# A gather-bound relational GNN kernel: paced gathers, other end groups, an earlier start of layer 2, shared node-block transfers

## Chip, cores, metric

The kernel runs on one core of one Trainium2 chip. The metric is the device time of one execution in microseconds; 3947.32 us is the median of ten runs before the change.

## The reference

N = 12500 nodes with C = 128 channels, E = 200000 edges sorted by destination, ten relations. The type of an edge is the argmax of ten of its 42 attributes. Two layers follow, then a residual and a layer norm (no scale or shift):

```python
def _rgcn_layer(x, src, dst, edge_type, w_rel, root, bias):
    N = x.shape[0]
    seg = dst * NUM_REL + edge_type
    xs = x[src]
    sums = jax.ops.segment_sum(xs, seg, num_segments=N * NUM_REL)
    cnt = jax.ops.segment_sum(jnp.ones(seg.shape, x.dtype), seg, num_segments=N * NUM_REL)
    mean = (sums / jnp.maximum(cnt, 1.0)[:, None]).reshape(N, NUM_REL, -1)
    return jnp.einsum('nrd,rdo->no', mean, w_rel) + x @ root + bias
h = jax.nn.relu(_rgcn_layer(x, src, dst, edge_type, w_rel1, root1, b1))
out = _layernorm(x + _rgcn_layer(h, src, dst, edge_type, w_rel2, root2, b2))
```

## The kernel before

The edges are cut into 1563 tiles of 128. A layer goes over them in groups: 95 groups of 16 tiles, then seven end groups of 8, 8, 8, 8, 4, 4 and 3. For each tile GpSimd issues one indirect DMA (L466) that gathers 128 rows of 512 bytes, one for the source of each edge, from x in layer 1 and from the hidden table hD in layer 2. VectorE makes a weighted one-hot matrix `oh` of the tile (L481: relation and place of the destination in a window of 12 nodes, weight one over the count), and TensorE multiplies the two into PSUM (zp, L495). ScalarE copies a group's zp out (zs, L509). For each half of 8 tiles TensorE projects with the ten relation matrices (L521); ScalarE copies (ms, L525 and L527); TensorE places the half's rows into a window of 160 nodes (L537), and VectorE adds that window to `acc`, the transposed node sums, at an offset read from memory (L543). In full groups projection and add run one and two groups behind the gathers; in end groups everything is projected and added at once.

The gathers are queued on GpSimd in tile order. They write a ring of three buffers of 16 tiles (`gpool`). Their completion goes over eight semaphores in turn, so each gather waits for the gather eight places before it, and the first of a group also for TensorE to have finished with its buffer. In full groups the first zp matmul waits for all 16 gathers.

Layer 1 also prepares the edges, in 13 chunks of 128 tiles, as steps between its groups: `sources` (L167) loads and transposes the indices, `types` (L286) loads the attributes in two halves of a chunk of 1.344 MB each (L303, on SyncE's queue, into buffers m0 and m1) and takes the argmax (L279 to L284), writes keys to memory, and `count` (L340) reads them back shifted and counts equal neighbours on VectorE and TensorE (L362 to L366). A half's buffer is loaded again, for the next chunk, once VectorE's L281 has read it.

Nodes are finished in 29 blocks: 23 of 512, then 128s, the last of 84. `done_after` says after which group a block has all its edges. `block_in` (L394) loads x, in layer 2 also hD, through SyncE (`rows_dma`, L392) and transposes it (L407, L409). `block_rows` (L412) adds the bias to the sums (L416), clears `acc` for layer 2 (L418), multiplies with the root matrix (L421) and adds the sums, transposed by a matmul with the identity (L422). `hidden` (L429) applies relu (L435) and stores to hD. `final` (L438) adds the residual x (L447) and normalises (L450 to L457). Layer 2's first gather reads hD, so it waits for the stores of all 29 blocks. In layer 2 a flag is computed (L628 to L640) that sends unusual edge lists to a general path behind the two layers; with these inputs it isn't taken.

Of the kernel before, what the change touches and what calls it, by code (L numbers as in the profile page):

```python
# [20 lines left out]
P = 128  # L21
# [10 lines left out]
RING = 3  # L32
DB = 8
# [10 lines left out]
def rgcn_resnorm_kernel(ctx: ExitStack, tc: tile.TileContext, x, src, dst, attr, w_rel1, root1, b1,  # L44
# [25 lines left out]
    while t < NT:  # L70
        groups.append((t, min(HT if NT - t > 3 * QB else QB, NT - t)))
        t += groups[-1][1]
# [15 lines left out]

    HALF = NT * P - E
    assert C == P and E % GT == 0 and 0 < HALF < P and NT % CT and 1 < groups[-1][1] < groups[-2][1]  # L90
# [27 lines left out]
    wE = keep.tile([P, NCH * CT], F32, name="wE")  # L118

# [46 lines left out]

    def sources(c):  # L167
        p = chunk_rows(c)
        s_i = prep.tile([P, P], I32, name="s_i")
        rows_from(s_i, src, c, 0, P)  # L170
        s_f = prep.tile([P, P], F32, name="s_f")
        early(c, nc.vector.tensor_copy(s_f[:p], s_i[:p]))
        return to_edges(idxE, s_f, c)
# [112 lines left out]
    def types(c):  # L286

        p = chunk_rows(c)
        last = c == NCH - 1
        d_i = prep.tile([P, P + L + 1], I32, name="d_i")  # L290
        if last:
            nc.vector.tensor_copy(d_i[:p, P:], pads[:p])
            q = p - 1
            nc.sync.dma_start(d_i[:q], bass.AP(dst.tensor, dst.offset + c * CE, [[P, q], [1, P + L + 1]]))
            nc.sync.dma_start(d_i[q:p, :P], bass.AP(dst.tensor, dst.offset + E - P, [[P, 1], [1, P]]))
        else:
            rows_from(d_i, dst, c, 0, P + L + 1)
        n = p - 1 if last else p
        ty = prep.tile([P, P], F32, name="ty")
        H = P // 2  # L300
        for o in (0, H):
            m = prep.tile([P, H * D], F32, name=f"m{o // H}")
            d = nc.sync.dma_start(m[:n], bass.AP(attr.tensor, attr.offset + (c * CE + o) * D, [[P * D, n], [1, H * D]]))  # L303
            if last:
                nc.sync.dma_start(m[n:p], bass.AP(attr.tensor, attr.offset + (E - P + o) * D,
                                                  [[P * D, 1], [1, H * D]]))
            if c == 1:
                later(d)
            argmax(c, ty[:p, o:o + H], m[:p].rearrange("p (j d) -> p j d", d=D)[:, :, EMB:EMB + NREL], p, H, prep,
                   riotaP, topP[o // H])  # L310
            yield
        d_f = prep.tile([P, P + L + 1], F32, name="d_f")
        early(c, nc.vector.tensor_copy(d_f[:p], d_i[:p]))
        k = prep.tile([P, P], F32, name="k")
        nc.vector.scalar_tensor_tensor(k[:p], d_f[:p, :P], float(NREL), ty[:p], op0=ALU.mult, op1=ALU.add)
        o = L + c * CE
        nc.sync.dma_start(KD[0, o:o + n * P].rearrange("(p e) -> p e", e=P), k[:n])
        if last:
            nc.sync.dma_start(KD[:, L + E - P + HALF:L + E], k[n:p, HALF:])
        yield  # L320
        key = prep.tile([P, P], F32, name="key")
        nc.vector.tensor_scalar(key[:p], d_f[:p, :P], d_f[:p, 0:1], None, op0=ALU.subtract)
        nc.vector.scalar_tensor_tensor(key[:p], ty[:p], float(WN), key[:p], op0=ALU.mult, op1=ALU.add)
        to_edges(keyE, key, c)
        yield

        bad = prep.tile([P, P], F32, name="bad")
        far = prep.tile([P, P], F32, name="far")
        nc.vector.tensor_tensor(bad[:p], d_f[:p, 1:P + 1], d_f[:p, :P], op=ALU.is_lt)
        nc.vector.tensor_tensor(far[:p], d_f[:p, L + 1:], d_f[:p, :P], op=ALU.is_equal)  # L330
        nc.vector.tensor_tensor(bad[:p], bad[:p], far[:p], op=ALU.max)
        f = prep.tile([P, 2], F32, name="f")
        nc.vector.tensor_reduce(f[:p, 0:1], bad[:p], axis=AX.X, op=ALU.max)
        nc.vector.tensor_tensor(f[:p, 1:2], d_f[:p, P - 1:P], d_f[:p, 0:1], op=ALU.subtract)
        nc.vector.tensor_scalar(f[:p, 1:2], f[:p, 1:2], float(WN) - 0.5, None, op0=ALU.is_gt)
        nc.vector.tensor_reduce(f[:p, 0:1], f[:p], axis=AX.X, op=ALU.max)
        nc.vector.tensor_tensor(fl[:p], fl[:p], f[:p, 0:1], op=ALU.max)
        yield
# [44 lines left out]
    def rows_dma(sb, dr, k, store):  # L383
        n0, n, _ = block(k)
        full = n // P
        pairs = []
        if full:
            pairs.append((sb[:, :full], dr[n0:n0 + full * P, :].rearrange("(t p) c -> p t c", p=P)))
        if n % P:
            pairs.append((sb[:n % P, full], dr[n0 + full * P:n0 + n, :]))  # L390
        for a, b in pairs:
            then("SP", nc.sync.dma_start(b, a) if store else nc.sync.dma_start(a, b))  # L392

    def block_in(k, l):  # L394

        n0, n, subs = block(k)
        last = "e" if k == NBLK - 1 else ""
        b = len(subs) if last else 4
        xb = fin.tile([P, b, C], F32, name="xb" + last)
        rows_dma(xb, x, k, False)  # L400
        fb = xb
        if l:
            fb = fin.tile([P, b, C], F32, name="hb" + last)
            rows_dma(fb, hD, k, False)
        pt = ps_f.tile([P, YB], F32, name="pf")
        for t, h in subs:
            nc.tensor.transpose(pt[:, t * P:t * P + h], fb[:h, t, :], ident[:h, :h])  # L407
        fT = fin.tile([P, b * P], F32, name="fT" + last)
        nc.scalar.activation(fT[:, :n], pt[:, :n], AF.Copy)  # L409
        return xb, fT  # L410

    def block_rows(fT, k, l):  # L412

        n0, n, subs = block(k)
        a = fin.tile([P, YB], F32, name="a")
        nc.vector.tensor_scalar(a[:, :n], acc[:, n0:n0 + n], bsb[l], None, op0=ALU.add)  # L416
        if l == 0:
            nc.vector.memset(acc[:, n0:n0 + n], 0.0)  # L418
        pr = ps_f.tile([P, 4, C], F32, name="pf")
        for t, h in subs:  # L420
            nc.tensor.matmul(pr[:h, t, :], fT[:, t * P:t * P + h], rsb[l], start=True, stop=False)  # L421
            nc.tensor.matmul(pr[:h, t, :], a[:, t * P:t * P + h], ident, start=False, stop=True)  # L422
        return pr
# [5 lines left out]
    def hidden(k, ready):  # L429

        xb, fT = ready
        pr = block_rows(fT, k, 0)
        hb = fin.tile([P, 4, C], F32, name="hb")
        for p, s in spans(k):
            nc.scalar.activation(hb[:p, s], pr[:p, s], AF.Relu)  # L435
        rows_dma(hb, hD, k, True)

    def final(k, ready):  # L438

        xb, fT = ready  # L440
        pr = block_rows(fT, k, 1)
        v = fin.tile([P, 4, C], F32, name="v")
        mv = small.tile([P, 4, 2], F32, name="mv")
        rstd = small.tile([P, 4], F32, name="rstd")
        _, n, subs = block(k)
        for p, s in spans(k):
            nc.vector.tensor_tensor(v[:p, s], pr[:p, s], xb[:p, s], op=ALU.add)  # L447
# [7 lines left out]
        o = fin.tile([P, 4, C], F32, name="o")  # L455
# [3 lines left out]
        rows_dma(o, out, k, True)  # L459
# [3 lines left out]

    def gather(table, t0, n):
        g = gpool.tile([P, G, C], F32, name="g")
        return g, [then("POOL", nc.gpsimd.indirect_dma_start(  # L466
            out=g[:, j, :], out_offset=None, in_=table, in_offset=bass.IndirectOffsetOnAxis(
                ap=idxE[:, t0 + j:t0 + j + 1], axis=0))) for j in range(n)]

    whole = mybir.DependencyInfo(mybir.DependencyClass.Sync, mybir.DependencyReason.DATA)  # L470
# [4 lines left out]
    def ones(k):  # L475

        t0, n = groups[k]
        oh = dpool.tile([P, G, KW], F32, name="oh")
        for j in range(n):
            t = t0 + j  # L480
            then("DVE", nc.vector.tensor_scalar(oh[:, j, :], iotaP[:, :KW], keyE[:, t:t + 1], wE[:, t:t + 1],  # L481
# [4 lines left out]
        return oh, at  # L486

    def sums(table, k, oh, at):
# [4 lines left out]
        zp = ps_z.tile([P, G // QB, YB], F32, name="zp")  # L493
        for j in range(n) if end else reversed(range(n)):
            m = nc.tensor.matmul(zp[:, j // QB, j % QB * KW:(j % QB + 1) * KW], g[:, j, :], oh[:, j, :],  # L495
                                 start=True, stop=True)
# [48 lines left out]
    def layer(table, l, finish, steps, flag_too=False):  # L545
# [8 lines left out]
        def add_oldest():  # L554
# [3 lines left out]
            while done < NBLK and sum(groups[k]) >= done_after(done):  # L558
                finish(done, ready if done == NBLK - 1 else given or block_in(done, l))
# [3 lines left out]
        for k in range(NG):  # L563
            end = k >= NS
            if k and not given and done < NBLK - 1:
                given = block_in(done, l)
            if projected:
                add_oldest()
            if end:
# [4 lines left out]
                if not ready:  # L574
                    ready = block_in(NBLK - 1, l)
# [6 lines left out]
            held.append(sums(table, k, *(made or ones(k))))  # L582
            made = ones(k + 1) if end and k < NG - 1 else None
# [27 lines left out]
    zero = fin.tile([P, YB], F32, name="a")  # L611
    nc.vector.memset(zero, 0.0)
    for a in range(0, NPAD, YB):
        m = min(NPAD - a, YB)
        nc.scalar.activation(acc[:, a:a + m], zero[:, :m], AF.Copy)
# [3 lines left out]
    weights_in()  # L619
    todo = []  # L620
    for c in range(1, NCH):
        s = [as_steps(sources, c + 1)] if c + 1 < NCH else []
        todo.append((c * CT // G - 2, [8 + L // DB + 2], chain(*s, types(c), count(c))))
# [22 lines left out]

    gp = ctx.enter_context(tc.tile_pool(name="gp", bufs=2))
# [120 lines left out]
    with tc.If(flag > 0):  # L768
# [3 lines left out]
        for l, (table, finish) in enumerate(((x, hidden), (hD, final))):  # L772
            nc.vector.memset(acc, 0.0)
# [29 lines left out]
```

## Time and profile before

| | us |
|---|---|
| median of 10 runs (lowest to highest) | 3947.32 (3944.27 to 3949.68) |
| the profiled execution | 3952.98 |
| its span in the profile | 3951.2 |
| first gather of layer 1, last gather of layer 1 | 4.3, 1962.0 |
| first gather of layer 2, last gather of layer 2 | 1973.7, 3928.4 |
| GpSimd busy | 2963.8 (75%) |
| TensorE matmul busy | 2337.4 (59%) |
| VectorE busy | 1512.0 (38%) |
| granted TensorE clock, mean | 0.78 |

How to read it: PE is TensorE, PEld its weight loads, DVE VectorE, ACT ScalarE, POOL GpSimd, SP SyncE; a q behind the name (POOLq, SPq) is that engine's queue of instructions, where DMAs are issued. A group's row gives line, engine and operation, then "output<-inputs", the count, and times; what stands behind "idle" or in brackets is the time in which the engine did nothing before the instruction, and what ended it. "issue" means that the profile shows nothing it waited for. The chain of waits follows the work that ended last backwards, step by step, to what released it. Timeline rows begin with start and duration in us. "DMA to landing" is the time from an issue to the end of its transfer.

### The profile page before, as it was taken

To read this page: it belongs to the slowest core of one execution; us is meant where nothing else is said; L and a number is where in the kernel's file an instruction comes from. 1 tells how busy PE (TensorE), PEld (TensorE's weight loads), DVE (VectorE), ACT (ScalarE), POOL (GpSimd) and SP (SyncE) were. 2 spreads that over 40 slices of the span, in tenths; PEclk is the share of its full clock that TensorE was granted. 3 is DMA by queue.
4 is the path that set the end of the run, shared out by engine and by line. 5 is a ranking of instruction groups with operands and counts; after the bars stand their busy time and mean duration, and the time that the engine had idled before them with its cause. 6 is when DMAs were issued, how large, how long until landed. Compare 5 with 4: busy or idle time off the path is not lost.

```text
span 3951.2 us, 43799 instructions
## 1 busy us (share of the span) xinstructions
PE 2337.4 (59%) x16206; PEld 2245.4 (57%) x16206; DVE 1512.0 (38%) x4660; ACT 528.8 (13%) x1142; POOL 2963.8 (75%) x3142
## 2 busy tenths in 40 slices
PE   4656565565666656656745565555655565556556
PEld 4655555565555555555635565555555555556556
DVE  6444444343444434443323333333333333333333
ACT  2111111111111111111101111111111111111111
POOL 7777777777777777777677777777777777777775
PEclk8777777777777777777877777777777777777778
DMA  5222322222222222221222222222222222222221
GB/s 163 89 73 75 94 59 90 88 65 89 74 74 93 61 89 64 63 62 56 63 58 58 61 69 61 61 61 62 68 61 61 61 69 61 61 61 69 61 59 55
DMA packets 180538, 278.99 MB, mean 71 GB/s; under 512 B 55608, under 2 KB 127175, under 8 KB 177191
## 3 DMA queue, kind: packets, MB, share of 16 engines
q0 software_dynamic: 100032, 205.07, 18.2%
q1 hardware_dynamic: 78577, 71.03, 5.6%
q8 instruction: 132, 2.16, 0.2%
q14 instruction: 89, 0.73, 0.1%
q10 hardware_dynamic: 1708, 0.01, 0.0%
HBM read 262.28 MB, written 13.60 MB: 70 GB/s over the span
## 4 chain that ended last, share of the span: by engine, by line
POOL 66%; issue 24%; DMA 7%; PE 2%; ACT 0%; DVE 0%; POOLq 0%; SPq 0%; ACTq 0%
POOL g L466 66%; DMA g<-in_x_dram,idxE 3%; DMA g<-hD,idxE 3%; PE pp L521 1%; PE zp L495 1%; PE pp L537 0%; ACT zs L509 0%; PE pf L422 0%; PE pf L421 0%; DMA xb<-in_x_dram 0%; POOLq L466 0%; DVE acc L543 0%; DVE a L416 0%; PE pf L407 0%; ACT ms L527 0%
## 5 line engine op out<-in xcount | busy, mean ns | idle before, releaser
L495 PE MATMUL zp<-oh,g 128*128 128x120 f32 x6252 | 1137.8, 358 | 1538.0 <-DMA g<-hD,idxE 789.8
L495 PEld LDWEIGHTS zp<-oh,g 128*128 128x128 f32 x6252 | 1097.3, 271 | 1576.5 <-issue 1474.3
L466 POOL DMA_INDIRECT g<-hD,idxE x1563 | 1478.7, 946 | 487.6 <-issue 470.5
L466 POOL DMA_INDIRECT g<-in_x_dram,idxE x1563 | 1482.4, 948 | 477.2 <-issue 457.7
L481 DVE TENSOR_SCALAR oh<-bank,keyE,wE 128x120 f32<-128x120 f32 x3126 | 1004.0, 400 | 717.4 <-PE zp L495 717.0
L521 PE MATMUL pp<-w,zs 128*96 128x128 f32 x7880 | 898.9, 273 | 17.5 <-ACT zs L509 14.3
L521 PEld LDWEIGHTS pp<-w,zs 128*96 128x96 f32 x7880 | 871.0, 163 | 23.4 <-ACT zs L509 18.5
L509 ACT ACTIVATE zs<-zp 128x480 f32<-128x480 f32 (+1 forms) x782 | 386.0, 575 | 2522.9 <-PE zp L495 2522.6
L543 DVE TENSOR_TENSOR acc<-acc,pp 128x160 f32 x204 | 65.5, 321 | 1390.7 <-PE pp L537 1390.4
L537 PE MATMUL pp<-at,ms 96*128 96x160 f32 (+1 forms) x788 | 210.8, 407 | 6.9 <-ACT ms L527 5.1
L537 PEld LDWEIGHTS pp<-at,ms 96*128 96x128 f32 (+1 forms) x788 | 171.0, 271 | 23.0 <-ACT ms L527 15.9
L527 ACT ACTIVATE ms<-pp 96x256 f32<-96x256 f32 (+1 forms) x198 | 74.5, 376 | 451.0 <-PE pp L521 451.0
L485 DVE TENSOR_SCALAR at<-bank,place 96x160 f32<-96x160 f32 x394 | 133.6, 375 | 0.0
L362 DVE TENSOR_TENSOR eqb<-pf,kh 128x1344 bf16<-128x1344 f32 (+2 forms) x65 | 100.5, 1552 | 75.5 <-PE pf L366 67.9
L422 PE MATMUL pf<-ident,a 128*128 128x128 f32 x392 | 81.4, 291 | 2.1 <-DVE a L416 1.9
L421 PE MATMUL pf<-root,fT 128*128 128x128 f32 x388 | 79.0, 287 | 1.3 <-ACT fT L409 1.3
L422 PEld LDWEIGHTS pf<-ident,a 128*128 128x128 f32 x392 | 64.6, 207 | 3.4 <-DVE a L416 3.1
L421 PEld LDWEIGHTS pf<-root,fT 128*128 128x128 f32 x388 | 62.9, 204 | 2.1 <-ACT fT L409 2.1
L435 ACT ACTIVATE hb<-pf 128x512 f32<-128x512 f32 (+2 forms) x29 | 15.4, 531 | 331.2 <-PE pf L422 329.0
L364 PE MATMUL pf<-eqb,identb 128*128 128x512 bf16 (+2 forms) x130 | 50.5, 389 | 10.6 <-DVE eqb L362 10.6
L366 PE MATMUL pf<-eqb,identb 128*128 128x512 bf16 (+2 forms) x130 | 50.8, 391 | 0.0
L447 DVE TENSOR_TENSOR v<-pf,xb 128x512 f32<-128x512 f32 (+1 forms) x28 | 17.4, 620 | 74.0 <-PE pf L422 73.8
(107 smaller groups left out, 454.7 us busy)
## 6 DMA issues: line engine op xcount, KB each, us to landing
m<-in_edge_attr_dram SPq DMA_DIRECT2D x24, 1344.0 KB
g<-in_x_dram,idxE POOLq DMA_INDIRECT x1563, 2.5
g<-hD,idxE POOLq DMA_INDIRECT x1563, 2.5
xb<-in_x_dram SPq DMA_DIRECT2D x46, 256.0 KB
hD<-hb SPq DMA_DIRECT2D x23, 256.0 KB
hb<-hD SPq DMA_DIRECT2D x23, 256.0 KB
out_dram<-o SPq DMA_DIRECT2D x23, 256.0 KB
w<-in_L_gnn_w_rel_dram SPq DMA_DIRECT2D x2, 640.0 KB
```

What stands on the lines that cost most here:

```text
L362: nc.vector.tensor_tensor(eq[:p], kp[:p, None, :R].to_broadcast([p, DB, R]), fore, op=ALU.is_equal)
L421: nc.tensor.matmul(pr[:h, t, :], fT[:, t * P:t * P + h], rsb[l], start=True, stop=False)
L422: nc.tensor.matmul(pr[:h, t, :], a[:, t * P:t * P + h], ident, start=False, stop=True)
L466: return g, [then("POOL", nc.gpsimd.indirect_dma_start(out=g[:, j, :], out_offset=None, in_=table, in_offset=bass.IndirectOffsetOnAxis(ap= ...
L481: then("DVE", nc.vector.tensor_scalar(oh[:, j, :], iotaP[:, :KW], keyE[:, t:t + 1], wE[:, t:t + 1], op0=ALU.is_equal, op1=ALU.mult))
L485: nc.vector.tensor_scalar(at[:, h, :], iotaP[:HR], place[:, h, k:k + 1], None, op0=ALU.is_equal)
L495: m = nc.tensor.matmul(zp[:, j // QB, j % QB * KW:(j % QB + 1) * KW], g[:, j, :], oh[:, j, :], start=True, stop=True)
L509: then("ACT", nc.scalar.activation(zs[:, :, b * QB:b * QB + m, :], zp[:, b, :m * KW].rearrange("c (j r n) -> c r j n", r=NREL, n=WN), AF.C ...
L521: nc.tensor.matmul(po[:m * WN, h], zs[:, r, h * HT:h * HT + m].rearrange("c j n -> c (j n)"), wsb[l][:, r, :], start=(r == 0), stop=(r == ...
L527: nc.scalar.activation(ms[:, :n // HT], po[:HR, :n // HT], AF.Copy)
L537: nc.tensor.matmul(pa, ms[:m * WN, h], at[:m * WN, h], start=(h == 0), stop=(h == len(parts) - 1))
L543: nc.vector.tensor_tensor(acc[:, s], acc[:, s], pa, op=ALU.add)
```

## The change

1. A gather whose tile number is 6 modulo 8 waits for the landing of the gather three places before it. All gathers are given their order as dependencies without a semaphore.
2. The end groups are 8, 8, 8, 12 and 7 tiles.
3. The first 16 gathers of layer 2 read only the first 12288 rows of hD (`EARLY`, blocks 0 to 26), with indices clamped to them (`idxH`) and weight zero (`wH`) for edges from later rows. What these edges carry is added by eight matmuls (`late_sums`) from the hidden rows of the last two blocks, kept in SBUF (`late_h`), and matrices that `head` prepares at the end of layer 1 (`late_w`).
4. `hidden` also computes layer 2's root product, bias and residual and puts them into `acc`, so layer 2 loads no node blocks and `final` only transposes `acc` and normalises. `acc` starts at b1 in place of zero.
5. Transfers: two blocks of 512 nodes share one load of x, one store to hD and one store of the output (512 KB each); the indices of four chunks share a load; a chunk's attributes come in one load of 2.69 MB in place of two (the first chunk keeps two).

```diff
-        groups.append((t, min(HT if NT - t > 3 * QB else QB, NT - t)))
+        n = NT - t
+        groups.append((t, HT if n > 2 * HT + QB else HT + QB if n > HT + QB else n))
...
+    def of_four(c, a, name, n):
+        if c == 0 or c == NCH - 1:
+            return prep.tile([P, n], I32, name=name)
+        if c % 4 == 1:
+            q = min(4, NCH - 1 - c)
+            four[name] = prep.tile([P, 4, n], I32, name=name + "4")
+            nc.sync.dma_start(four[name][:, :q], bass.AP(a.tensor, a.offset + c * CE, [[P, P], [CE, q], [1, n]]))
+        return four[name][:, (c - 1) % 4]
...
+        m = prep.tile([P, P * D], F32, name="m")
         for o in (0, H):
-            m = prep.tile([P, H * D], F32, name=f"m{o // H}")
-            d = nc.sync.dma_start(m[:n], bass.AP(attr.tensor, attr.offset + (c * CE + o) * D, [[P * D, n], [1, H * D]]))
+            w = H if c == 0 else P
+            if w == H or not o:
+                d = nc.sync.dma_start(m[:n, o * D:(o + w) * D], bass.AP(
+                    attr.tensor, attr.offset + (c * CE + o) * D, [[P * D, n], [1, w * D]]))
...
-    def rows_dma(sb, dr, k, store):
+    def rows_dma(sb, dr, k, store, name=None):
         n0, n, _ = block(k)
+        if k < NPAIR:
+            if k % 2 != store:
+                return
+            n0, n, sb = starts[k - k % 2], 2 * YB, halves_of[name]
...
+    def hidden(k, fT):
+        n0, n, subs = block(k)
+        pr = ps_f.tile([P, 4, C], F32, name="pf")
+        for t, h in subs:
+            nc.tensor.matmul(pr[:h, t, :], fT[:, t * P:t * P + h], rsb[0], start=True, stop=False)
+            nc.tensor.matmul(pr[:h, t, :], acc[:, n0 + t * P:n0 + t * P + h], ident, start=False, stop=True)
+        i = k - (NBLK - 2)
+        hb = late_h[:, i:i + 1] if i >= 0 and not anew else half(k, "hb")
         for p, s in spans(k):
             nc.scalar.activation(hb[:p, s], pr[:p, s], AF.Relu)
+        rows_dma(hb, hD, k, True, "hb")
+        pt = ps_f.tile([P, YB], F32, name="pf")
+        for t, h in subs:
+            nc.tensor.transpose(pt[:, t * P:t * P + h], hb[:h, t, :], ident[:h, :h])
+        hT = fin.tile([P, YB], F32, name="hT")
+        nc.scalar.activation(hT[:, :n], pt[:, :n], AF.Copy)
+        po = ps_f.tile([P, YB], F32, name="pf")
+        nc.tensor.matmul(po[:, :n], rsb[1], hT[:, :n], start=True, stop=True)
+        nc.vector.scalar_tensor_tensor(acc[:, n0:n0 + n], po[:, :n], bsb[1], fT[:, :n], op0=ALU.add, op1=ALU.add)
...
+    def final(k, _):
+        n0, n, subs = block(k)
+        v = ps_f.tile([P, 4, C], F32, name="pf")
...
+        for t, h in subs:
+            nc.tensor.matmul(v[:h, t, :], acc[:, n0 + t * P:n0 + t * P + h], ident, start=True, stop=True)
...
+    def head():
+        nc.vector.tensor_scalar(idxH, idxE[:, :G], EARLY - 1, None, op0=ALU.min)
...
+        for b in range(0, G, QB):
+            pm = [ps_f.tile([P, YB], F32, name="pf") for _ in range(2)]
+            for j in range(QB):
+                t = b + j
+                oh = prep.tile([P, KW], F32, name="ohH")
+                nc.vector.tensor_scalar(oh, iotaP[:, :KW], keyE[:, t:t + 1], wE[:, t:t + 1],
+                                        op0=ALU.is_equal, op1=ALU.mult)
+                for i in range(2):
+                    of = prep.tile([P, P], F32, name=f"of{i}")
+                    nc.vector.tensor_scalar(of, iotaP[:, :P], off[:, i, t:t + 1], None, op0=ALU.is_equal)
+                    nc.tensor.matmul(pm[i][:, j * KW:(j + 1) * KW], of, oh, start=True, stop=True)
...
     def gather(table, t0, n):
         g = gpool.tile([P, G, C], F32, name="g")
+        ix = idxE
+        if is_head(table, t0):
+            table, ix = table[:EARLY, :], idxH
+        for j in range(n):
+            d = then("POOL", nc.gpsimd.indirect_dma_start(
+                out=g[:, j, :], out_offset=None, in_=table, in_offset=bass.IndirectOffsetOnAxis(
+                    ap=ix[:, t0 + j:t0 + j + 1], axis=0)))
+            if (t0 + j) % PACE == PACE - 2 and len(begun) > 2:
+                tc.add_manual_dep(d.ins, begun[-3].ins.name, whole, reason="no more than three under way")
+            if begun:
+                tc.add_manual_dep(d.ins, begun[-1].ins.name, behind, reason="gathers in their order")
+            begun.append(d)
+        return g, begun[-n:]
...
+    def late_sums(table, t0, banks):
+        if is_head(table, t0):
+            for b, z in enumerate(banks):
+                for i in range(2):
+                    n = block(NBLK - 2 + i)[1]
+                    nc.tensor.matmul(z[:, :QB * KW], late_h[:n, i, :], late_w[i][:n, b * QB * KW:(b + 1) * QB * KW],
+                                     start=(i == 0), stop=False)
```

## The prediction

> **What bounds the kernel now.** I read the page's busy shares and its chain of waits first, then the answer for the gather line L466, then the timeline around the turn between the layers, around a load of the edge attributes and at the end. Page, busy shares and chain:
>
> ```profile
> PE 2337.4 (59%) x16206; PEld 2245.4 (57%) x16206; DVE 1512.0 (38%) x4660; ACT 528.8 (13%) x1142; POOL 2963.8 (75%) x3142
> ...
> POOL 66%; issue 24%; DMA 7%; PE 2%; ACT 0%; DVE 0%; POOLq 0%; SPq 0%; ACTq 0%
> ```
>
> POOL and the issue gap before its instructions are 90% of the chain. The gather line says why 75% busy is nevertheless full:
>
> ```profile
> L466 POOL DMA_INDIRECT g<-in_x_dram,idxE x1563: 942/947/1387, 4.3 to 1962.0; - x196
> L466 POOL DMA_INDIRECT g<-hD,idxE x1563: 942/947/1143, 1973.7 to 3928.4; - x196
> ...
>   issue: 928.2, 3010
>   DMA g<-in_x_dram,idxE: 17.4, 57
>   DMA g<-hD,idxE: 16.2, 53
> ...
> DMA to landing us min/median/max: 2.4/2.5/6.8
> ```
>
> A gather takes 0.947 us, and 928.2/3010 = 0.31 us of issue lies before it; so one starts every 1.25 us, 3126 times. The waits on earlier gathers (57 and 53) cost 17.4/57 = 0.31 us each, no more than the ordinary gap: a satisfied wait is free. Layer 1 takes 1962.0 − 4.3 = 1957.7 us (1562 intervals at 1.2533) and layer 2 1954.7. The rest of the span is 4.3 before the first gather, 11.7 at the turn and 3951.2 − 3928.35 = 22.85 after the last gather. PE, DVE and ACT matter only at turn and tail, or where they hold up POOL.
>
> **The turn.** Timeline, layer 1's last block and layer 2's first gathers:
>
> ```profile
> 1971.41 0.33 SPq L392 DMA_DIRECT2D hD<-hb  x1
> ...
> 1973.71 0.95 POOL L466 DMA_INDIRECT g<-hD,idxE  x1 [10.72 <-issue]
> 1974.96 0.95 POOL L466 DMA_INDIRECT g<-hD,idxE  x1 [0.30 <-issue]
> ```
>
> POOL stands idle 10.72 us until the last hidden block is stored; the ordinary gap is 0.30. In the change the first 16 gathers read only blocks 0 to 26, stored by about 1951, over 10 us earlier, so 10.72 − 0.30 = **−10.4 us**. What is late next is the second group, 16 × 1.25 = 20 us later; it needs the last store, issued now 9.4 us after layer 1's last gather. The eight matmuls that supply the messages of blocks 27 and 28 lie on PE, 59% busy. DVE's 48 extra operations for their weights (16 of the 0.40 us of an L481 row, 32 no wider than that: under 20 us) lie in the last three groups, 60 us at 38% busy. If that cover fails, the ring of three buffers gives POOL 48 gathers before it feels it.
>
> **The tail.** Timeline of the last 23 us:
>
> ```profile
> 3928.35 0.94 POOL L466 DMA_INDIRECT g<-hD,idxE  x1 [0.30 <-issue]
> ...
> 3939.66 2.38 PE L521 MATMUL pp<-w,zs 128*36 128x128 f32 x20 [0.62 <-ACT zs L509]
> ...
> 3942.97 0.32 DVE L543 TENSOR_TENSOR acc<-acc,pp 128x160 f32 x1 [3.98 <-PE pp L537]
> 3943.32 0.27 DVE L416 TENSOR_SCALAR a<-acc,b 128x84 f32<-128x84 f32 x1
> ...
> 3944.13 0.29 DVE L447 TENSOR_TENSOR v<-pf,xbe 84x128 f32<-84x128 f32 x1 [0.54 <-PE pf L422]
> 3944.45 0.29 DVE L450 BATCH_NORM_STATS2 st<-v 84x6 f32<-84x128 f32 x1
> ```
>
> The last three groups (4, 4, 3 tiles) each pay a projection of 2.4 us one after another on PE, and the last begins 11.3 us after the last gather. With 12 and 7, the 12 are gathered 8.75 us before the last gather X, and their projection (two halves, 2 × 2.4) ends before X. For the 7: landing X+2.5, last four zp matmuls 0.7, copy 0.57, projection 2.4, copy 0.27, two matmuls 0.54 and hops of about 0.4 give acc at X+7.4 against X+14.6 now: −7.2. From acc to the statistics is 1.48 now; the bias add and the residual add go, so about 0.84: −0.6. The 7 can still queue behind the 12's last adds on PE, so I take **−7** (bounds −8 and −5).
>
> **Smaller gains.** The memsets L418 (29) and the bias adds L416 (58) go, as do layer 2's block loads (29 of hD, 29 of x). A gather beside such an operation is longer: 1.14 us at 2118.78, 1.20 at 952.37. With 0.2 us for some ten of them, **−1.5** (0 to −3). In layer 1 each hidden block gains four transposes and one wide matmul (an L421 matmul is 0.29 us) and one DVE operation; PE has 41% idle and 48 gathers of ring, so 0. The one wait on PE that POOL shows beyond a gap is 0.9 us (PE zp, 1.2 in 2): left at 0. The larger block transfers (512 KB) and index loads lie on SP and in the DMA queues. Their price is that gathers land later, which costs only through the next part.
>
> **The added wait.** One gather in eight, d, waits for the landing of the third last, d−3, 3.75 us before d is due. Behind it stand all later gathers, so a stall is lost for good. A released POOL starts about 0.3 us later (it started at 4.32 after an index written at 4.04). So d stalls when d−3 takes more than 3.75 − 0.3 = 3.45 us. The median is 2.5: most of the 390 waits are free. Slow ones come with the attribute loads. Timeline, and the gather line in the window 936 to 948:
>
> ```profile
> 936.99 0.33 SPq L303 DMA_DIRECT2D m<-in_edge_attr_dram  x1
> ```
> ```profile
> DMA to landing us min/median/max: 2.5/3.6/4.7
> ```
>
> By the completion events in the trace the load lands 6.13 us after issue, and gathers issued 0.3, 1.6, 2.9 and 4.1 us after it take 5.6, 4.7, 3.6 and 2.8: all land at about +6 to +7, when the load is over. Over layer 1, 135 gathers take more than 3.45 us, in layer 2 35. Of those in the place of a d−3, ten in layer 1 would cost 13.4 us together (28.8: 2.1; 38.8: 2.6; 58.8: 3.4; 279.7: 1.6; 459.9: 2.1; the others 0.6 or less), one in layer 2 0.2. The change merges the two loads of 1.344 MB of a chunk into one of 2.69 MB. From +2.9 to +6.13 us a load moves its bytes in some 3.2 us, so the merged one ends at about +9.4, and d−3 issued u after it costs about 6 − u. In the regular chunks (from 594 us on, six loads) the gather in that place now starts 4.1 to 4.5 us after the second half's load. In the changed order that load is freed four or five one-hot operations (0.40 each, L481) earlier in its group: u = 5.7 to 6.5, a cost between 0 and 0.3; unshifted 1.5 to 2.1 each. I take 0, since the operations' durations give it, and keep 2.1 for the range. What stays: the early loads, 4 (of the 8.1 above the second and third fall less far behind once POOL has waited, and one load of a chunk goes), and the chunk at 459, whose place is early in its load (u = 0.46 now, some 2 shifted): 4. **+8 in all** (bounds: 0, and 40, as worked out below).
>
> The Trainium skill ("DMA: Bandwidth & Descriptors", § Queues, rings and completion order) says that a DMA engine turns between its queues packet by packet. Here the first gather in a load took 5.6 us, almost to the load's end, so the trace shows much less sharing. By the rule a merged load would hold no gather longer than a half load does, and the added wait would stay near the 13.4 us of above, at 3941; the row's reading makes the cost depend on where the load falls.
>
> **Sum.** −10.4 − 7 − 1.5 + 8 = −10.9 on the profiled 3952.98 us, which is 3942.1; that execution stands 5.66 us above the median of the ten runs, so the median goes from 3947.32 to about 3936.5, taken as 3937.
>
> **Rivals.** A measurement of this kernel can tell about 0.2% (7.9 us) from no change.
> A, the forecast: gains of 18.9 and waits that cost 0 to 11: 3928 to 3939. If the waits are never felt, 3928.4. For it: satisfied waits are free, and a load every 160 us leaves most of the 390 untouched. 0.45.
> B, the paced gathers fall into the end of the regular loads (1.1 each, 6.6), the early ones cost 8 and the chunks at 171 to 459 6: about 20, and gain and loss cancel, 3948. For it: a shift of 1 us in u is enough, and 13.4 us come out of the landings as they are. 0.29.
> C, slower: the load is issued early in the ten microseconds before each d, so that d−3 stands at its head. A mean cost over places with u from 0 to 6 is 3 to 3.4 us; with eleven loads and 4 at the start about 40, so 3947.3 − 18.9 + 40 = 3968. It decides from (18.9 + 7.9 − 4)/11 = 2.1 us a load on. For it: today the chunk at 459 already has u = 0.46; against it: the six regular ones have 4.1 or more. 0.26.
> That the turn does not close (a store or the flag between the layers still waited for) would take 10 us back and leads to B or C from A.
> The range of 3927 to 3966 takes in A and B and most of C.
>
> **What would show it.** Right: the first gather from hD has an idle of about 0.3 us; acc's last add stands about 7.4 us after the last gather; POOL's idle on gathers exceeds 0.31 per wait by some 8 us in all, before 600 us; layer 1 takes 1962 to 1966 us, layer 2 about 1953. Wrong: gather stalls of 1 us and more after every load (B, C), a wait of POOL for PE early in either layer, or an issue gap that grows beyond 0.31 us at the paced gathers, which would cost 390 times what it is.

## The result: 14 us slower

The changed kernel takes 3961.53 us (median of 8 runs, 3960.54 to 3967.01), the kernel before 3947.51 (28 runs, 3943.87 to 3949.68): a ratio of 1.0039, 95% interval 1.0030 to 1.0048. The profiled execution took 3962.34 us with a span of 3960.3. The forecast was 3937.

Page of the changed kernel, busy shares and chain of waits:

```profile
PE 2391.9 (60%) x16104; PEld 2244.8 (57%) x16104; DVE 1514.6 (38%) x4621; ACT 535.7 (14%) x1148; POOL 2954.3 (75%) x3142
...
POOL 58%; issue 26%; DMA 14%; PE 2%; DVE 0%; POOLq 0%; ACT 0%; DVEq 0%; ACTq 0%
```

The busy shares tell nothing: all five engines are within a point or so of where they were. The chain does: POOL falls from 66% to 58% and DMA rises from 7% to 14%, and these are landings of gathers. The gather line, L541 in the changed kernel:

```profile
L541 POOL DMA_INDIRECT g<-in_x_dram,idxE x1563: 938/944/1255, 4.2 to 1983.4; - x196
L541 POOL DMA_INDIRECT g<-hD,idxE x1547: 939/944/961, 2004.6 to 3944.8; - x194
L541 POOLq EVENT_SEMAPHORE  x590: 17/17/43, 18.2 to 3938.5; - x197
...
its engine sat idle before it (us, times) until:
  issue: 889.6, 2887
  DMA g<-in_x_dram,idxE: 61.0, 110
  DMA g<-hD,idxE: 37.4, 121
```

Layer 1's last gather starts at 1983.4 in place of 1962.0. Of 61.0 us on 110 waits in layer 1, 110 ordinary gaps of 0.305 explain 33.6; 27.4 are stalls. In layer 2 the waits (37.4 on 121) are ordinary gaps. Adding up by how much each gather starts later than 1.2504 us (the ordinary interval) after the one before, the gathers with the wait ("paced" below) lose 27.4 us in layer 1 and 8.5 in layer 2, all others together less than nothing. The 8.5 stand under "issue".

Three places of the timeline. First the turn, POOL's rows, the last gather of layer 1 and the first of layer 2:

```profile
1983.41 0.94 POOL L541 DMA_INDIRECT g<-in_x_dram,idxE  x1 [0.30 <-issue]
1984.66 0.94 POOL L541 DMA_INDIRECT g<-hD,idxH  x1 [0.30 <-issue]
```

The idle of 10.72 us is gone: 0.30. Then the tail:

```profile
3944.76 0.94 POOL L541 DMA_INDIRECT g<-hD,idxE  x1 [0.30 <-issue]
...
3949.11 2.41 PE L613 MATMUL pp<-w,zs 128*84 128x128 f32 x20 [1.26 <-ACT zs L601]
...
3952.46 0.32 DVE L635 TENSOR_TENSOR acc<-acc,pp 128x160 f32 x1 [3.12 <-PE pp L629]
...
3953.33 0.29 DVE L488 BATCH_NORM_STATS2 st<-pf 84x6 f32<-84x128 f32 x1 [0.54 <-PE pf L485]
```

One projection after the last gather in place of a queue of them; the last add comes 7.7 us after the last gather (14.6 before), the statistics 0.87 after the add (1.48), and the kernel ends 15.6 us after the last gather (22.9). So both gains came. Last, a load of attributes and the paced gather behind it:

```profile
788.19 0.82 DVE L303 TENSOR_TENSOR eq<-m,bank 128x640 f32<-128x640 f32 x1
...
789.04 0.34 SPq L327 DMA_DIRECT2D m<-in_edge_attr_dram  x1
...
794.13 0.94 POOL L541 DMA_INDIRECT g<-in_x_dram,idxE  x1 [0.30 <-issue]
...
800.20 0.94 POOL L541 DMA_INDIRECT g<-in_x_dram,idxE  x1 [2.62 <-DMA g<-in_x_dram,idxE]
```

The load starts when VectorE's second argmax has read the buffer. The third last gather, at 794.13, goes out 5.1 us behind it and lands 5.81 us later, at 799.94; the paced gather was due at 797.88 and starts at 800.20. The six stalls from 638 to 1448 us look like this (1.6 to 2.3 us each, 12.0 us together), those at 190 to 476 cost 0.9, 3.3 and 2.9, the first 80 us 6.9. The load of the last, short chunk, at 1598.9, costs nothing.

The "issue" part of layer 2 is something else. POOL's rows of the timeline there:

```profile
2288.36 0.95 POOL L541 DMA_INDIRECT g<-hD,idxE  x1 [0.30 <-issue]
...
2290.86 0.94 POOL L541 DMA_INDIRECT g<-hD,idxE  x1 [0.30 <-DMA g<-hD,idxE]
2294.11 0.94 POOL L541 DMA_INDIRECT g<-hD,idxE  x1 [2.31 <-issue]
```

The paced gather is the one at 2294.11. The gather it waits for (2288.36) landed at 2290.79, and POOL's queue passed that wait at 2290.81; the gather was due at 2292.11 and came 2.0 us late with nothing that the profile shows to wait for. Such pauses stand at 2294, 2826, 3358 and 3890, 532 us apart. At all four the gather starts 3.28 us after the queue passed the wait; at a load's stall, as above, it starts 0.26 us after the landing.

In some of the runs below TensorE and not the gathers was the bound: the kernel before took 4630 to 4732 us beside them, and they have a section of their own.

**Theory 1:** the added wait is the whole loss: it takes away POOL's lead in its queue, so that a landing held up by a load, or a pause in the queue, stops the gathers. **Rivals:** the merged and larger transfers delay the gathers by themselves; the wait has a fixed price, whatever it waits for; the stalls at the loads come from the place of a load in its group and not from its length.

### The profile page after: what moved, and what is told of

It reads as the page before. It is cut to its first block, busy times and chain, and to the rows that moved or that the text cites. A ratio compares the mean times of both kernels' runs of the same rounds, so it can differ in the third digit from the quotient of the medians.

```text
span 3960.3 us, 43631 instructions
## 1 busy us (share of the span) xinstructions
PE 2391.9 (60%) x16104; PEld 2244.8 (57%) x16104; DVE 1514.6 (38%) x4621; ACT 535.7 (14%) x1148; POOL 2954.3 (75%) x3142
## 4 chain that ended last, share of the span: by engine, by line
POOL 58%; issue 26%; DMA 14%; PE 2%; DVE 0%; POOLq 0%; ACT 0%; DVEq 0%; ACTq 0%
POOL g L541 58%; DMA g<-hD,idxE 7%; DMA g<-in_x_dram,idxE 6%; PE zp L586 1%; PE pp L613 1%; PE pp L629 0%; POOLq L541 0%; PE pf L463 0%; DVE oh L562 0%; DMA g<-hD,idxH 0%; PE pf L462 0%; PE pf L475 0%; ACT zs L601 0%; PE pf L471 0%; DMA s_i<-in_src_dram 0%
## 5 line engine op out<-in xcount | busy, mean ns | idle before, releaser
L586 PEld LDWEIGHTS zp<-oh,g 128*128 128x128 f32 x6252 | 1115.1, 277 | 1460.0 <-issue 1420.3
L541 POOL DMA_INDIRECT g<-in_x_dram,idxE x1563 | 1476.6, 945 | 504.2 <-issue 441.3
L541 POOL DMA_INDIRECT g<-hD,idxE x1547 | 1459.7, 944 | 481.7 <-issue 444.0
L613 PE MATMUL pp<-w,zs 128*96 128x128 f32 x7840 | 923.5, 274 | 46.7 <-DVE acc L635 30.6
L629 PE MATMUL pp<-at,ms 96*128 96x160 f32 (+2 forms) x784 | 175.4, 352 | 50.8 <-ACT ms L619 50.2
L629 PEld LDWEIGHTS pp<-at,ms 96*128 96x128 f32 (+2 forms) x784 | 134.2, 219 | 81.4 <-ACT ms L619 75.0
L476 DVE SCALAR_TENSOR_TENSOR acc<-pf,b,fT 128x512 f32<-128x512 f32 (+1 forms) x28 | 19.0, 680 | 71.9 <-PE pf L475 71.9
L463 PE MATMUL pf<-ident,acc 128*128 128x128 f32 x196 | 45.6, 321 | 0.4 <-DVE acc L635 0.4
L462 PE MATMUL pf<-root,fT 128*128 128x128 f32 x194 | 44.4, 316 | 0.6 <-ACT fT L446 0.6
L463 PEld LDWEIGHTS pf<-ident,acc 128*128 128x128 f32 x196 | 37.6, 238 | 0.7 <-DVE acc L635 0.7
L462 PEld LDWEIGHTS pf<-root,fT 128*128 128x128 f32 x194 | 36.8, 236 | 1.2 <-ACT fT L446 0.8
```

Source lines behind the costliest of these rows:

```text
L462: nc.tensor.matmul(pr[:h, t, :], fT[:, t * P:t * P + h], rsb[0], start=True, stop=False)
L463: nc.tensor.matmul(pr[:h, t, :], acc[:, n0 + t * P:n0 + t * P + h], ident, start=False, stop=True)
L541: d = then("POOL", nc.gpsimd.indirect_dma_start(out=g[:, j, :], out_offset=None, in_=table, in_offset=bass.IndirectOffsetOnAxis(ap=ix[:, t ...
L613: nc.tensor.matmul(po[:m * WN, h], zs[:, r, h * HT:h * HT + m].rearrange("c j n -> c (j n)"), wsb[l][:, r, :], start=(r == 0), stop=(r == ...
L629: nc.tensor.matmul(pa, ms[:m * WN, h], at[:m * WN, h], start=(h == 0), stop=(h == len(parts) - 1))
```

## The experiments

"Late" below is again the start of a gather less 1.2504 us less the start of the one before, summed over the paced ones (tile number 6 modulo 8). The runs in which the gathers are the bound come first.

### Without the wait

```diff
-            if (t0 + j) % PACE == PACE - 2 and len(begun) > 2:
-                tc.add_manual_dep(d.ins, begun[-3].ins.name, whole, reason="no more than three under way")
```

> The full changed kernel without the added wait. Theory 1, with the lean runs: 36 to 42 us below the changed kernel's 3961.5, so 3920 to 3926, and 21 to 28 below the kernel before. Rival (TensorE's full work takes part of it back, at the block ends in layer 1): 3930 to 3945.

Measured: 3926.27 us (3925.68 to 3926.62), beside 3947.13 of the kernel before: 0.9946, interval 0.9932 to 0.9959. The gather line of this kernel:

```profile
L541 POOLq EVENT_SEMAPHORE  x201: 17/17/942, 57.0 to 3891.7; - x101
...
its engine sat idle before it (us, times) until:
  issue: 941.4, 3089
  DMA g<-in_x_dram,idxE: 5.5, 18
  DMA g<-hD,idxE: 3.7, 12
```

5.5/18 and 3.7/12 are the ordinary 0.31 us; 941.4/3089 is 0.305, so the pauses of layer 2 are gone too, and with them 389 of the 590 semaphore instructions. No gather starts over 0.4 us late in either layer. Merged loads, paired blocks and the rest are all in. The rival of the larger transfers falls: the wait costs 35 us (3961.5 − 3926.3), the profile had 35.9. The time is a little above the 3920 to 3926 expected, which were taken from the lean runs below. This version beats both kernels: its slowest run, 3926.62, is 18 us under the fastest of the kernel before, 3944.41.

### The attributes in two half loads again

The loop of the kernel before, with its buffers m0 and m1, in the changed kernel:

```diff
-        m = prep.tile([P, P * D], F32, name="m")
         for o in (0, H):
-            w = H if c == 0 else P
...
+            m = prep.tile([P, H * D], F32, name=f"m{o // H}")
+            d = nc.sync.dma_start(m[:n], bass.AP(attr.tensor, attr.offset + (c * CE + o) * D, [[P * D, n], [1, H * D]]))
```

> The full changed kernel with the wait, and a chunk's attributes in two half loads again. If the length of the load sets the stalls: those from 189 us on fall from 0.9 to 3.3 us each to under 1.7, layer 1's paced gathers are 8 to 14 us late in place of 27.4, layer 2's 8.5 stay, and the time is 3942 to 3950. If its place does: 3957 to 3965.

Measured: 3944.81 us (3943.09 to 3949.98) beside 3947.13: 0.9996, interval 0.9987 to 1.0005. Its gather line, L538 there:

```profile
  issue: 938.0, 3044
  DMA g<-in_x_dram,idxE: 22.0, 42
  DMA g<-hD,idxE: 9.3, 29
```

22.0 − 42 × 0.305 = 9.2 us of stalls in layer 1 in place of 27.4: 2.4, 2.2, 1.2 and 0.5 in the first 80 us, 2.7 at 311 where the third last gather goes out at the same moment as a load, and none of 0.5 or more after that. The six stalls from 638 us on are gone, and with the place unchanged: in front of each paced gather that stalled, the third last goes out 5.1 to 5.3 us behind the merged load, and here 5.1 us behind a half load. One of the six:

```profile
781.61 0.35 SPq L325 DMA_DIRECT2D m<-in_edge_attr_dram  x1
...
786.75 0.94 POOL L538 DMA_INDIRECT g<-in_x_dram,idxE  x1 [0.30 <-issue]
...
790.49 0.94 POOL L538 DMA_INDIRECT g<-in_x_dram,idxE  x1 [0.30 <-issue]
```

By the completion events the gather at 786.75 lands 2.5 us after its start, when the half load has been over for 1.4 us; the one at 794.13 above, in the same place behind a merged load, took 5.8. So in the regular places it is the length that counts. At 311 the place counts. Layer 2 keeps its 9.0, with pauses of 2.1 to 2.2 us at 2276, 2808, 3340 and 3872: it loads no attributes, and they have nothing to do with loads.

### Lean kernels: the gathers alone

All 16 tiles of a group are gathered and waited for, but only the first 8 are multiplied, and five of ten relations projected, so that the gathers are the bound whatever TensorE does:

```diff
-        for j in range(n) if end else reversed(range(n)):
+        for j in range(live) if end else reversed(range(live)):
...
-            for d in gathers[:j]:
+            for d in gathers[:j] + gathers[j + 1:]:
...
-            for r in range(NREL):
+            for r in range(0, NREL, 2):
```

with `live = min(n, HT)`, and copies, projection and add cut to it. In `fifth_lean` the paced gather waits for the fifth last:

```diff
-            if (t0 + j) % PACE == PACE - 2 and len(begun) > 2:
-                tc.add_manual_dep(d.ins, begun[-3].ins.name, whole, reason="no more than three under way")
+            if (t0 + j) % PACE == PACE - 2 and len(begun) > 4:
+                tc.add_manual_dep(d.ins, begun[-5].ins.name, whole, reason="no more than three under way")
```

> The changed kernel with most of TensorE's work left out, so that the gathers are the bound on any chip: all 16 tiles of a group are gathered and waited for, but only the first 8 are multiplied, copied, projected (relations 0, 2, 4, 6, 8) and added. Gathers, loads, waits, stores and VectorE's one-hots stay. Theory 1: as in the profile of the changed kernel, 24 to 30 us of late paced gathers in layer 1 and about 8 in layer 2, 1.25 us between the others, and about 3955 us.

> The same lean kernel without the added wait. Theory 1 (the wait is the whole loss): 30 to 40 us below the lean kernel with it, no paced gather late. Rival (merged loads and larger block transfers cost by themselves): less than 20 us below, with late gathers elsewhere.

> The kernel before, lean in the same way. By the steps (turn about 10 or a little less with the shorter chain, tail 4 to 7, shorter gathers 2 to 9) it lies 14 to 26 us above the lean changed kernel without the wait, so 8 to 22 below the one with it. Rival (the other parts gain nothing): within 5 us of the one without the wait.

> The lean changed kernel with the paced gather waiting for the fifth last in place of the third last. Theory 1: the gathers issued in a load all land at its end, so 15 to 22 us of layer 1 stay, and layer 2's pauses go: 8 to 20 us below the lean changed kernel. Rival (each wait has its price): the same time as the lean changed kernel, pauses included.

| lean form of | us | late in layer 1, layer 2 |
|---|---|---|
| the changed kernel | 3967.52 | 28.3, 9.5 |
| the same without the wait | 3925.07 | 0.8, 0.1 |
| the same, waiting for the fifth last | 3935.62 | 9.1, 0.3 |
| the kernel before | 3938.01 | 0.0, 0.0 |

(The full kernel before took 3947.36 beside these.) Gather line of the lean changed kernel, waits on gathers:

```profile
  DMA g<-in_x_dram,idxE: 48.6, 67
```

The lean kernel without the wait:

```profile
  DMA g<-in_x_dram,idxE: 8.8, 29
```

And with the wait for the fifth last:

```profile
  DMA g<-in_x_dram,idxE: 26.0, 56
  DMA g<-hD,idxE: 18.6, 61
```

Per wait that is 0.73, 0.30 and 0.46 us in layer 1. By the medians the wait costs 42 us here, over the 30 to 40 expected, and the lean changed kernel lies well over the 3955 expected of it. But the medians don't compare like with like. The runs of both lean kernels fall into two groups some 9 us apart (3959.0 and 3959.6 against 3967.5 to 3970.8; 3924.8 to 3926.1 against 3933.5), and the median is in the upper group for one and in the lower for the other. The profiled runs are in the upper groups and have a median gather of 947 ns, which in other runs is 944; 3126 × 0.003 = 9 us would be the distance. Upper against upper the wait costs 37 us (3970.83 − 3933.48), lower against lower 34: within the 30 to 40.

With more lead three of the four pauses of layer 2 are gone and the fourth is 0.7 us (0.3 late in all, 18.6/61 = 0.30 per wait), although there are as many paced gathers and as many semaphore instructions (590): the price isn't that of a wait as such, and the rival of the fixed price falls. It is the lead that counts: in the place of the fourth pause the queue passes the wait at 3328.59 and the gather starts at 3331.87, again 3.28 us later, and in the other three places it passes the wait 3.6 us or more before the gather is due. For layer 1 I had expected 15 to 22 us to stay, and 9.1 stay: the loads' stalls are 0.8 to 2.2 us each with the fifth last, and at some loads there is none. That doesn't refute the reason: by the completion events the fifth last lands only some 0.6 us before the third last (10.6 and 11.2 us after the load at 626.67). But the loads lie elsewhere in their groups in this kernel (the third last goes out 6.3 to 6.6 us behind the regular ones, in place of 5.1 to 5.3), so the 9.1 don't price a later place alone. The time is 32 us below the lean changed kernel by the medians (8 to 20 expected), 24 below its lower group. The kernel before is 12.9 us above the one without the wait by the medians, under the 14 to 26 expected, and 8.4 by the two profiled runs, both at 947 ns: the turn gives 9.0 (10.2 to 1.25), the tail takes 1.7 back (14.5 to 16.2), and the gathers give 1.2: where the projection is short, the larger end groups gain nothing.

### Where TensorE is the bound

In these runs the kernel before took 4630 to 4732 us. Each kernel is compared only with the kernel before beside it. The code of "without the wait" is the same as above, and one chip gave the kernel before 4631.28 us in one set of runs and 3947.36 in the next, so this isn't a lasting property of a chip (the run expected on "another chip" had the same one as the first). The edits: those of above in full form, the wait in one layer alone, and the kernel before with the wait alone (gathers in a loop as in the change):

```diff
+            if (t0 + j) % 8 == 6 and len(begun) > 2:
+                tc.add_manual_dep(d.ins, begun[-3].ins.name, whole, reason="no more than three under way")
```

> The changed kernel without the added wait, all else kept. Theory 1 (the wait is the whole loss: by the profile of after, the paced gathers start 27.4 us late in layer 1 and 8.5 in layer 2, and the other parts gain 10.4 at the turn, 7.3 at the tail and some 9 in slightly shorter gather intervals): about 3961.5 - 36 = 3926, between 3922 and 3932, and no gather starts over 1 us late. Rival (the merged loads and larger block transfers delay gathers by themselves, or the shorter gathers come from the wait): 3935 to 3955, with late gathers at the loads or intervals back at 1.250 us.

> The kernel before with only the added wait (and the gathers' order). Theory 1 (the wait costs by itself, even with the two half loads): the landings of before put 13.4 us of stalls on the gathers in that place in layer 1, and layer 2's pauses of 2 us without a releaser add 4 to 9: 3947.5 + 13 to 25 = 3960 to 3972. Rival (the cost needs the merged 2.69 MB load; with half loads the wait is nearly free): 3947 to 3953.

> The changed kernel with the wait in layer 1 alone. Theory 1 (layer 2's 8.5 us of late gathers come from the wait, though no landing is late there): 3961.5 - 8 = 3953, and no gather of layer 2 more than 0.5 us late. Rival (the four pauses of 2 us in layer 2 have another cause, and stay): 3961.

> The changed kernel with the wait in layer 2 alone. Theory 1: layer 1 loses its 27 us of stalls at the loads, layer 2 keeps about 8: 3934. Rival (layer 1's stalls move to another wait of the queue): 3942 to 3960.

> The changed kernel without the added wait, on another chip than the first time. Theory 1 (the wait is the whole loss; 27.4 + 8.5 us of late paced gathers go): 3926, between 3922 and 3932, at a granted clock near 0.78. Rival (something else in the change costs): 3935 to 3955.

> The kernel before with the added wait alone. Theory 1: 3960 to 3975, with 13 to 28 us of late paced gathers in layer 1 and 4 to 9 in layer 2. Rival (the merged load is needed for the loss): 3947 to 3953.

> The changed kernel, but the paced gather waits for the fifth last gather in place of the third last. Theory 1, loads: all gathers issued in a load land at its end, so waiting for an earlier one helps little: some 20 of the 27 us of layer 1 stay. Theory 1, layer 2: the queue may run 2.5 us further ahead, and the pauses of 2 us that no landing explains are hidden: 8.5 falls to under 2. Together about 3948 (3944 to 3953). Rival (the price is that of each wait, whatever it waits for): 3961, with the four pauses still there.

> The changed kernel with the attributes of a chunk loaded in two halves of 1.344 MB again. Theory 1 (the merged load holds the third last gather to about 11 us after its issue; a half load ends some 4 us earlier): the stalls of 1.6 to 3.3 us at the nine loads from 189 us on go or fall under 0.5, layer 1's 27 us become 6 to 12, and the time is about 3944 (3940 to 3948). Rival (the stalls come from the place of the load in its group, not its length): 3957 to 3962.

> The changed kernel without the added wait, to be measured where the multiplies run at the pace of the first profiles (273 ns for an L521 matmul; 347 in the two calls before, which made TensorE the bound). Theory 1 (the wait is the whole loss): 3926 to 3935 beside 3947.5 of before. Rival (something else in the change costs as well): 3940 to 3955. If the multiplies are slow again, TensorE is the bound and the time says only what the change costs there: about 4795.

| kernel | us | kernel before, beside it | ratio, interval | late in layer 1, layer 2 |
|---|---|---|---|---|
| without the wait | 4793.36 | 4732.18 | 1.0132, 1.0114 to 1.0151 | 0.2, 0.0 |
| before with the wait | 4730.78 | 4732.18 | 0.9996, 0.9980 to 1.0011 | 28.1, 8.7 |
| wait in layer 1 alone | 4799.62 | 4732.18 | 1.0143, 1.0128 to 1.0159 | 12.0, −0.4 |
| wait in layer 2 alone | 4804.61 | 4732.18 | 1.0141, 1.0122 to 1.0159 | −0.4, 8.6 |
| without the wait, again | 4796.55 | 4726.59 | 1.0158, 1.0135 to 1.0180 | 0.0, 0.0 |
| before with the wait, again | 4733.82 | 4726.59 | 1.0017, 0.9998 to 1.0035 | 34.7, 8.2 |
| fifth last | 4814.32 | 4726.59 | 1.0188, 1.0163 to 1.0213 | 4.7, −0.4 |
| half loads | 4784.18 | 4726.59 | 1.0129, 1.0108 to 1.0151 | 9.5, 10.2 |
| without the wait, third time | 4751.21 | 4629.55 | 1.0264, 1.0246 to 1.0281 | −0.4, −0.4 |

The times expected took the gathers as the bound, and none came: these runs don't price the wait. The gather line of the kernel without the wait (second time) says why:

```profile
  issue: 868.3, 2816
  remote: 505.9, 145
  PE zp L583: 286.6, 39
```

POOL stands at the first gather of nearly every group ("remote" is a release that the profile can't name; both kinds fall on those gathers): a group takes about 23.2 us in place of 20.0. The multiplies themselves are not slower: a projection matmul takes 273 to 276 ns in the mean where the granted clock is 1.0, here as in the run of 3926 us. But half of them fall into stretches at 0.5, where they take 419 to 422, so that the mean is 337 to 348 ns; in the profiles of the two kernels at 3926 and 3947 us almost none do. And PE stands idle for 884 us before projection matmuls with nothing that the profile shows to wait for, which it never does in the run of 3926 us. What causes the two stays open. What can be read are the late starts, and they agree with theory 1: they come with the wait, layer by layer, and layer 2's pauses (four of 2.0 us where the wait is in layer 2) are gone where it isn't, or where it is for the fifth last. And here the wait costs nothing that can be told (0.9996 and 1.0017 for the kernel before with it, with 28 to 35 + 8 us of late starts): what a gather loses, POOL would have lost at the next group anyway. In the kernel before, with half loads, the wait was late by 28 us and more in layer 1, but its stalls there lie on gathers that slow groups have shifted; its price where the gathers bind wasn't measured.

Halving the projection alone (the third diff line of the lean kernels) was meant to free the gathers there:

> The changed kernel with half of the projection left out: only relations 0, 2, 4, 6 and 8 are multiplied, 20 matmuls a group in place of 40, so that TensorE isn't the bound even where an L521 matmul takes 347 ns; the gathers bound the kernel again, and everything on their path (loads, waits, stores) is as in the changed kernel. Theory 1: paced gathers start 24 to 30 us late in layer 1, at the early loads and at each 2.69 MB load, and 8 us late in layer 2: about 3955 to 3965.

> The same without the added wait (half of the projection left out too). Theory 1 (the wait is the whole loss): 30 to 40 us below the run with the wait, no gather over 0.5 us late for another gather. Rival (the merged loads or larger block transfers cost by themselves): less than 20 us below.

> The kernel before with half of the projection left out. By the sum of the steps (turn 10.4, tail about 6 with the shorter projection, 2 to 9 in shorter gathers) it lies 17 to 26 us above the changed kernel without the wait, and 10 to 18 us below the changed kernel with it. Rival (the turn or the tail doesn't gain where the projection is short): under 12 us above the one without the wait.

They took 4689.31, 4701.98 and 4615.75 us beside 4631.28 of the full kernel before. A group still took 22.9 us with 20 matmuls fewer, so they compare nothing that was asked. Why half the projection freed so little stays open.

## Why the prediction was wrong

The turn: forecast −10.4; the gap went from 11.67 to 1.25 us, −10.4. Right.

The tail: forecast −7; 22.87 to 15.59, −7.3. Right, by the steps given, with the 7's adds a little late (acc at 7.7 in place of 7.4): the 12's projection, which the prediction had ended before the last gather, ends some 0.2 us after it. In the kernel without the wait it ends 2.4 us after it, and the tail is 17.7: there it gains 5.2, near the bound of 5 that was given for this queueing.

Smaller gains: forecast −1.5. The gathers other than the paced ones gained 8.7 us from profile to profile, but that is as good as no effect of the change: the median gather takes 944 ns in this profile and 947 in that of before, and which one it is changes between executions of one kernel (947 in two of the four profiles of the kernel without the wait, 944 in the other two). 3126 × 0.003 = 9 us. At 947 ns, the lean kernel without the wait has 3.4 and 0.3 us in its layers over 1.2504 per gather, the full kernel before 4.6 and 1.5, the lean one 2.7 and 2.2: −2.4 or −1.2, within the bounds of 0 to −3. That the memsets and bias adds are behind it wasn't tested.

The added wait: forecast +8, measured 27.4 + 8.5 = 35.9. This is the step that failed, and all of the error is in it: with the wait never felt the prediction gave 3928.4, and the kernel without it takes 3926.3. (That these agree within 2 us is in part luck: the tail gains less there, and 9 us between executions lie in the gathers.) It failed in three terms. At the regular loads "a cost between 0 and 0.3", taken as 0: 12.0 for six. I had the third last gather at u = 5.7 to 6.5, it was at 5.1 to 5.3: in five of the six the load came only 0.7 to 1.0 us earlier in its group and not 1.6 to 2.0. (The sixth is a misreading: before, the gather at the load of 616.9 stood at 3.2 and not at 4.1 to 4.5.) And I had it land with the load's end at +9.4, and it lands at +10.4 to +10.9: the load line, which knows the landing of two loads, says

```profile
DMA to landing us min/median/max: 9.5/9.9/10.3
```

and the gathers behind it come in one after another up to 1 us after that. Together that is about 2 us a load, on a slope of "6 − u" that I took to be at its zero. Second, 4 for the chunk at 459 and nothing for its neighbours, measured 7.1 for the three at 190, 314 and 476; and 4 for the start, measured 6.9. Third, layer 2, of which the prediction said that "one in layer 2" would cost 0.2: four pauses of 2 us. They can't be seen in the landings of before at all, nor as a gap there: in the trace of before POOL's queue passes the wait at a group's start some five or six gathers ahead, 6 us and more, and 3.28 us fit into that. In the changed kernel it passes a paced wait 1.25 us ahead in the median. I counted what the wait would cost by landings alone, not what the lead had been good for. The prediction named the case ("an issue gap that grows"), but only as a price per wait.

Of the rivals, C had the right sign and nearly the size (40 for 35.9 us of waits, 3968 for 3961.5), and the price per load from which it decides, 2.1 us, is what the nine loads from 178 us on cost in the mean. The nearness is luck in part: the loads' 27.4 us lie between B's 20 and C's 40, and the 8.5 of layer 2 are in neither. C's mechanism, a third last gather at the head of a load, holds at 314 us (it went out 0.2 us ahead of the load, 3.3 us lost); at most loads the gather stands at half the load's length, and the end of the load is late enough. That the merged load made it so is shown by the half loads (27.4 to 9.2).

The Trainium skill's turn of a DMA engine between queues packet by packet ("DMA: Bandwidth & Descriptors", § Queues, rings and completion order) would have the merged load hold a gather no longer than a half load does. In this trace a gather issued 2.6 us behind the merged load took 7.9 us, one issued 2.6 us behind a regular half load 3.8 to 4.4 (the kernel with half loads), and the longest landing in the gather line went from 6.8 us (before) to 8.0. The measurement decides: the length of the load counts.

What makes the pauses of 2 us is open. They recur every 424 gathers, fall on the paced gather and cost nothing once the wait leaves 3.28 us of lead. That the supply of POOL's instructions is behind them would fit, but no run shows it: at two of the four the trace has no transfer on its "instruction" queues in the 14 us before.

## What to carry to other kernels

A wait that is satisfied at nearly every landing of the trace can still cost: it takes the lead of the queue, and whatever that lead was covering comes to light. So look for what a queue's run-ahead hides, not only for the landings of the transfer that is waited for. And where a cost depends on two times being within a microsecond of each other, take the middle of its bounds, not the end that one row suggests: six loads at the zero of a slope were 12 us.

## What the hardware showed that I had not expected

One and the same kernel has its median gather at 944 ns in one execution and at 947 in another, through both layers: 9 us of 3950.

Where TensorE is the bound the changed kernel without the wait is 1.3 to 2.6% slower than the kernel before, where it is 0.5% faster otherwise. Layer 1 then ran from 4 to 2446 us against 2359 in the kernel before with the wait, layer 2 took 2285 us against 2313. That the work which the change moved from layer 2's blocks into layer 1's costs more there than it saves would fit; no run takes it apart.
